# A graph layer on a sparse matrix: rows of A a unit ahead, list products before the addition, later stores, fewer open tiles, lists in pieces

## The chip, the cores and the metric

The kernel runs on one core of one Trainium2 chip. The metric is the device time of one launch in microseconds (us). The core has five engines with a queue of instructions each: PE (TensorE: matrix products and transposes), DVE (VectorE), ACT (ScalarE), POOL (GpSimd) and SP (SyncE, which only starts transfers and passes semaphores). Transfers between HBM and the on-chip memory run on 16 DMA engines; SP, ACT and POOL can ask for them. Products accumulate in eight PSUM banks of 128 x 512 fp32.

## The reference

With A the 4096 x 4096 input `adj`, x of shape 8 x 4096 x 256 and a 256 x 256 weight:

```python
HW = einsum('bnf,fo->bno', x, W)
A_norm = relu((A + A.T) * 0.5)
D = sum(A_norm, axis=1)
d = where(D > 0, D ** -0.5, 0)
L_norm = eye(N) - d[:, None] * A_norm * d[None, :]
out = relu(einsum('nm,bmo->bno', L_norm, HW))
return layernorm(x + out)          # over the last axis, eps 1e-5
```

A is sparse, and denser towards low node numbers: an entry (i, j) is kept with a chance that falls with both numbers. Where a block of A has no entry in a row, the product of that row can be left out.

## The kernel before

The nodes are cut into 32 blocks of 128 (NB). Every fp32 matmul stands in the trace as two records.

**The forming stage** runs over pairs (i, j) of 512 x 512 blocks, i from 0 to 7 and j from i to 7. For each pair two blocks of A are loaded on SP's queue (L455), transposed on PE (L465), added on DVE (`symmetrise`, L469), scaled and clipped on ACT (`keep`, L473) and written to `a_dram` on ACT's queue (L485). `keep` also sums each run of 32 columns on DVE (L476, `sums`); POOL marks which runs have an entry (`uses`, L477), and adds the runs in four halvings to one sum per row (L482 and L484, `part`), from which `degrees` makes the row factors. Between these, `form` multiplies x by W (L568, L579), scales it to g, writes it to `g_dram`, and `multiply` (L537) adds the dense first row block, `lead`. Nothing here is pinned to an order but by a few explicit dependencies: a planner orders each engine's instructions ahead of time. A list `due` holds work on lists, counted down once per pair (i, j) by `run_due`.

**Lists.** For every unit u, two row blocks 2u+1 and 2u+2 (the last has one), the kernel decides on the chip which nodes go where. `patterns` (L213) finds for every node which of the eight 32-column strips of the unit it touches; each pattern is a kind (KINDS). `count` and `count_rest` multiply these marks by triangular matrices on PE, `place` and `place_rest` turn the counts into slots on DVE (a scan, L205 to L210, then offers of overflow from one kind to another, L298 to L301, then the slot, L311 to L339), `spread` makes one-hot matrices, `collect` multiplies them, and `index` (L410 to L426) reads the resulting node numbers, `gi` and `ai`. CAPS gives how many half tiles of 64 nodes each kind has in each unit, FIRST at which half tile it begins. Both are constants; L186 and L187 write them to `limit` and `base` with one POOL memset for each unit and kind.

**The gathering stage** runs over units in the order SEQ. The first two or three node blocks (HUBS) are kept: their rows of g stay in `hubs`, and for each unit `load_hub_rows` loads their rows of A (`gh`, 128 x 256) on POOL's queue. All other nodes come in tiles of 128: `gather` (L904) asks for the tile's rows of A (`ga`, L910) and of g (`g`, L918) by indirect DMA into a ring of 11 slots, freed in order. `steps_of` lays out the products: a step is either one whole product (128 x 128, four matmuls over 2048 columns), or a round of up to eight products of 64 x 32, one per place of the array, taken from at most REACH open tiles. Two row blocks have four PSUM banks each, tag `b0` for the first and `b1` for the second. Within a round the two row halves of the array take turns at a bank; SP passes a tick from one quarter of the round to a later one (L1183), in SP's queue.

In this stage every engine keeps the order in which the code writes it (`queue`, `issue_after`). After each step `gather_ahead` refills free slots, and `run_later(2)` counts work that was put off down by two and runs what has come to two or less. When a row block is complete, `finish` has ACT evict it (L730), into one buffer `y`; `rest` then adds the residual and takes statistics on DVE (L740 to L768), `end` normalises (L773), and `store_late` stores on SP (L783). The residual lies in one of four buffers, which are loaded on ACT's queue (L724, `residuals`) and are free again when the store has landed. When the first row block of a unit is complete, `lists` runs the list products of later units on PE (two `b0` banks), and `read(False)` lets DVE read them (index, then both scans); `prepare` makes the one-hot matrices for the next.

Of the kernel before, what the change touches and what calls it, by code (L numbers as in the profile page):

```python
# [47 lines left out]
    [3, 6, 10, 13, 0, 22, 19, 24, 27, 16, 30, 50, 47, 44, 33],  # L48
    [9, 0, 6, 12, 3, 21, 27, 16, 24, 18, 42, 32, 40, 30, 34],
    [3, 8, 5, 11, 0, 25, 14, 20, 17, 23, 36, 38, 28, 30, 32],  # L50
    [3, 11, 8, 0, 6, 19, 24, 21, 14, 17, 26, 28, 35, 30, 32],
    [5, 7, 0, 9, 2, 12, 17, 20, 23, 15, 31, 26, 33, 30, 28],
    [12, 3, 6, 9, 0, 17, 14, 19, 24, 22, 28, 33, 32, 31, 29],
    [0, 2, 4, 7, 10, 14, 16, 19, 22, 25, 28, 29, 30, 31, 32],
    [9, 11, 6, 3, 0, 18, 23, 21, 14, 16, 26, 28, 30, 27, 29],
    [5, 3, 10, 7, 0, 21, 14, 18, 12, 16, 24, 26, 28, 27, 25],
    [3, 10, 8, 5, 0, 15, 17, 12, 19, 22, 24, 26, 27, 28, 25],
    [0, 4, 7, 9, 1, 18, 12, 14, 20, 17, 28, 24, 25, 26, 27],
    [3, 10, 4, 0, 7, 12, 19, 15, 22, 18, 26, 28, 27, 30, 29],
    [4, 6, 0, 2, 8, 17, 12, 10, 14, 19, 24, 20, 22, 23, 21],  # L60
    [8, 6, 4, 2, 0, 12, 16, 18, 10, 14, 20, 24, 22, 21, 23],
    [0, 2, 4, 6, 8, 10, 12, 14, 16, 18, 20, 20, 20, 21, 22],
    [0, 4, 8, 12, 16, 20, 20, 20, 20, 20, 20, 20, 20, 20, 20],
# [4 lines left out]
def kernel(  # L68
# [25 lines left out]
    nc = tc.nc  # L94
# [16 lines left out]
    REACH = 8  # L111
    LATE = 10
# [61 lines left out]
    carry = const.tile([P, NL, NB], F32, name="carry")  # L174
# [8 lines left out]
    for k in range(NL):  # L183
        nc.gpsimd.memset(kinds[:, k : k + 1], float(codes[k]))
        for u in range(NU):
            nc.gpsimd.memset(limit[:, u, k : k + 1], float(CAPS[u][k] * L))  # L186
            nc.gpsimd.memset(base[:, u, k : k + 1], float(FIRST[u][k] * L + 1))  # L187
# [78 lines left out]
    def place(u, tot, low):  # L266
# [36 lines left out]
        every = slice(None)  # L303
        for h in range(2):
            offer(0, (every, h), pairs)
# [3 lines left out]
        nc.vector.tensor_copy(upper[:, singles], upto[:, 2])  # L309
        fits = ipool.tile([P, NL, NB], F32, tag=f"incl{NL * NB}", name=f"fits_{u}", bufs=1)  # L310
# [129 lines left out]
    with (  # L440
# [10 lines left out]
        strips = holds.enter_context(tc.tile_pool(name="strips", bufs=8))  # L451
# [20 lines left out]
        def keep(i, j, sym, diag):  # L472
            nc.scalar.activation(sym, sym, AF.Relu, scale=0.5)  # L473
            rows = slice(i * A, (i + 1) * A)
            sums = stat1.tile([P, A, S // E], F32, tag="sums", name=f"sums_{i}_{j}", bufs=4)
# [4 lines left out]
            half = S // E // 2  # L480
            while half > 1:
                nc.gpsimd.tensor_add(sums[:, :, :half], sums[:, :, :half], sums[:, :, half : 2 * half])  # L482
                half //= 2
            nc.gpsimd.tensor_add(part[:, rows, j : j + 1], sums[:, :, :1], sums[:, :, 1:2])  # L484
# [144 lines left out]

        def count_place(u):  # L630
            tot = psum.tile([P, NL * NB], F32, tag="b0", name=f"tot_{u}")
            low = psum.tile([P, NL * NB], F32, tag="b0", name=f"low_{u}")
            count(u, tot, low)
            run(place(u, tot, low))
# [23 lines left out]
        for i in range(NS):  # L658
            diag = stat1.tile([P, A, P], F32, tag="diag", name=f"diag_{i}")
            for j in range(i, NS):  # L660
# [29 lines left out]
                run_due()  # L690
# [5 lines left out]
            if i == 1:  # L696
                for n, u in enumerate(SEQ[:2]):
                    patterns(u)
                    due += [[2 + n, count_place, (u,)], [4 + n, count_place_rest, (u,)]]
                due.sort(key=lambda d: d[0])  # L700
            elif i == 2:
                for n, u in enumerate(SEQ[2:4]):
                    patterns(u)
                    due.append([1 + n, count_place, (u,)])
                due.append([3, count_place_rest, (SEQ[2],)])
            elif i < 5 and i > 2:

                pieces = spread_early(SEQ[i - 3])
                for n in range(5):
                    due.append([1 + n // 2, next, (pieces, None)])  # L710
                due.append([4, collect_index, (SEQ[i - 3],)])
# [143 lines left out]
    with (  # L855
# [13 lines left out]
        hub_rows = [apool.tile([P, 2 * P], F32, tag=f"h{h}", name=f"gh{h}") for h in range(max(HUBS))]  # L869
# [22 lines left out]
        def load_hub_rows(units, h):  # L892

            u = next((v for v in units if HUBS[v] > h), None)
            if u is None:
                return
            with queue("pool"):
                nc.gpsimd.dma_start(
                    hub_rows[h], a_dram[h * P : (h + 1) * P, (2 * u + 1) * P : (2 * u + 3) * P]
                )  # L900
            got[u, -1 - h] = (hub_rows[h], hubs[h], P)
# [49 lines left out]
        for h in range(max(HUBS)):  # L951
            with queue("pool"):
                nc.gpsimd.dma_start(hubs[h], g_dram[h * P : (h + 1) * P, :])
            load_hub_rows(SEQ, h)
# [54 lines left out]
        def finish(i):  # L1009
# [24 lines left out]
            after(1, rest)  # L1034
# [24 lines left out]
        def lists(u):  # L1059
# [31 lines left out]
            after(1, read, False)  # L1091
# [18 lines left out]
        def product(u, op, c, ps, cols, start, stop):  # L1110

            t, _, b, _ = op
            at, gt, apart = got[u, t]
# [12 lines left out]
        for q, (u, step) in enumerate(steps):  # L1126
# [58 lines left out]
            for op in step:  # L1185
                t = op[0]
                uses_left[u, t] -= 1
                if t < 0 and not uses_left[u, t]:
                    load_hub_rows(SEQ[SEQ.index(u) + 1 :], -1 - t)
            gather_ahead()  # L1190
            run_later(2)
            for b in touched:
                if not any(left[b, e] for e in range(QU)):
                    finish(2 * u + 1 + b)
                    if b == 0:
                        after(2, lists, u)
        while later:
# [64 lines left out]
```

## Time and profile before

| what | us |
|---|---|
| median of 3 runs (lowest, highest) | 1694.35 (1692.22, 1695.94) |
| the profiled execution, its own time | 1692.59 |
| its span in the trace | 1690.8 |
| forming stage, up to the first product of L1116 | 616.6 |
| gathering stage, up to the end of PE's last product | 1050.6 |
| end (evictions, normalisation, last stores) | 23.6 |

| product group of L1116 | records | mean ns of one |
|---|---|---|
| 64 x 32 and whole, from the ring (`py<-g,ga`) | 7192 | 615 |
| whole, kept blocks (`py<-g_hub,gh`) | 592 | 643 |

The 7784 records of L1116 are the gathering stage. Their mean duration isn't the price of one, since up to eight run side by side; the price of a step is read from the timeline. In rows of the profile, the name before `<-` is what is written and the names behind it what is read; L-numbers are lines of the kernel printed above. A wait row names the engine and line that waited, what it waited for, the total in us, how often, and the longest. An engine's idle time matters only where the engine, or one that waits for it, sets the end.

### The profile page before, as it was taken

The numbers are of one execution on the slowest core, as the hardware profiler recorded it, in microseconds if no ns is written. First come the engines' busy times: TensorE is split into PE (matmuls) and PEld (weight loads), VectorE is DVE, ScalarE is ACT, GpSimd is POOL, SyncE is SP. The second block draws the span as 40 slices with busy tenths as digits, with TensorE's granted clock in tenths as the row PEclk, the third lists the DMA queues.
The fourth block names the chain that finished last, engine by engine and source line by source line (L and its number), as shares of the span: only waits on it lengthen the run. The fifth ranks groups of instructions, "written<-read, shape, count | busy, mean of one in ns | idle before, by whom it ended". The sixth has DMA issues, their size and how long they took to land.

```text
span 1690.8 us, 29762 instructions
## 1 busy us (share of the span) xinstructions
PE 1448.1 (86%) x11176; PEld 768.9 (45%) x11176; DVE 1022.9 (60%) x3071; ACT 367.2 (22%) x462; POOL 768.1 (45%) x1490
## 2 busy tenths in 40 slices
PE   5999989898889877989889789698999868879894
PEld 4788866676666632323223333243333323323331
DVE  4665689895464630092745938668047973975636
ACT  3555544444444510001010000100010010011002
POOL 5123121223233355656455375563546455647561
PEclk9999989999999988999999899898999979989997
DMA  8999999999888988889797788977859896999994
GB/s 309 373 368 399 386 342 339 353 319 362 299 301 320 367 319 311 342 308 367 280 357 285 276 307 300 368 278 290 331 209 384 287 359 223 333 341 357 353 385 146
DMA packets 217160, 546.74 MB, mean 323 GB/s; under 512 B 19035, under 2 KB 107403, under 8 KB 182955
## 3 DMA queue, kind: packets, MB, share of 16 engines
q0 software_dynamic: 54624, 286.49, 45.0%
q1 hardware_dynamic: 93472, 126.89, 21.9%
q10 hardware_dynamic: 68912, 131.37, 20.7%
q8 instruction: 91, 1.49, 0.3%
q14 instruction: 61, 0.50, 0.1%
HBM read 442.89 MB, written 136.34 MB: 343 GB/s over the span
## 4 chain that ended last, share of the span: by engine, by line
PE 46%; DVE 20%; DMA 17%; issue 8%; POOL 7%; ACT 2%; POOLq 0%; SPq 0%; ACTq 0%; DVEq 0%
PE py L1116 28%; PE pg L579 8%; DMA gh<-a_dram 5%; DMA g<-g_dram,gi 5%; PE lead L537 4%; DMA a_dram<-sym 4%; DVE sym L469 3%; DVE sums L476 2%; POOL g L918 2%; PE xtr L568 2%; PE tr L465 2%; POOL ga L910 2%; DMA ga<-a_dram,ai 2%; DVE stats L749 2%; DVE xr L773 1%
## 5 line engine op out<-in xcount | busy, mean ns | idle before, releaser
L1116 PE MATMUL py<-g,ga 64*32 64x512 f32 (+1 forms) x7192 | 603.7, 615 | 65.7 <-DMA g<-g_dram,gi 51.4
L1116 PEld LDWEIGHTS py<-g,ga 64*32 64x32 f32 (+1 forms) x7192 | 216.3, 113 | 440.0 <-issue 350.4
L910 POOL DMA_INDIRECT ga<-a_dram,ai x264 | 270.1, 1023 | 283.4 <-PE py L1116 218.1
L1116 PE MATMUL py<-g_hub,gh 128*128 128x512 f32 x592 | 293.1, 643 | 81.2 <-DMA gh<-a_dram 56.5
L918 POOL DMA_INDIRECT g<-g_dram,gi x264 | 292.6, 1108 | 103.6 <-issue 73.0
L740 DVE TENSOR_TENSOR xr<-xr,y 128x2048 f32<-128x2048 f32 x31 | 71.0, 2290 | 421.9 <-ACT y L730 421.9
L730 ACT ACTIVATE y<-py,minus_r 128x512 f32<-128x512 f32 x120 | 78.3, 687 | 958.3 <-PE py L1116 944.1
L579 PE MATMUL pg<-w_sb,xt 128*128 128x256 f32 x1024 | 232.7, 385 | 7.8 <-ACT xt L569 6.7
L1116 PEld LDWEIGHTS py<-g_hub,gh 128*128 128x128 f32 x592 | 115.8, 204 | 252.5 <-issue 148.6
L469 DVE TENSOR_TENSOR sym<-tr,adj 128x512 f32<-128x512 f32 x256 | 162.6, 682 | 93.7 <-PE tr L465 73.7
L579 PEld LDWEIGHTS pg<-w_sb,xt 128*128 128x128 f32 x1024 | 195.9, 194 | 36.4 <-ACT xt L569 7.1
L476 DVE TENSOR_REDUCE sums<-sym 128x64 f32<-128x2048 f32 x64 | 145.4, 2279 | 66.5 <-ACT sym L473 66.5
L465 PE MATMUL tr<-ident,adj 128*128 128x128 f32 x1024 | 140.2, 286 | 40.6 <-DVE sym L469 26.6
L473 ACT ACTIVATE sym<-sym 128x2048 f32<-128x2048 f32 x64 | 122.5, 1915 | 147.4 <-DVE sym L469 132.7
L477 POOL TENSOR_SCALAR uses<-sums 128x64 uint8<-128x64 f32 x64 | 28.1, 439 | 273.4 <-DVE sums L476 228.7
L465 PEld LDWEIGHTS tr<-ident,adj 128*128 128x128 f32 x1024 | 119.1, 146 | 72.3 <-DVE sym L469 41.7
L568 PE MATMUL xtr<-ident,xin 128*128 128x128 f32 x512 | 72.7, 286 | 20.5 <-DVE sym L469 19.3
L749 DVE BATCH_NORM_STATS2 stats<-xr 128x6 f32<-128x256 f32 x256 | 87.0, 412 | 1.1
L773 DVE TENSOR_SCALAR xr<-xr,mv,root 128x256 f32<-128x256 f32 x248 | 85.1, 415 | 0.1
L537 PE MATMUL lead<-gt,strip 128*128 128x512 f32 x176 | 83.0, 598 | 0.0
L569 ACT COPY xt<-xtr 128x512 f32<-128x512 f32 x128 | 68.0, 590 | 46.5 <-PE xtr L568 45.6
L589 ACT ACTIVATE gt<-pg,r 128x512 f32<-128x512 f32 x88 | 60.6, 688 | 75.0 <-PE pg L579 72.8
(153 smaller groups left out, 997.4 us busy)
## 6 DMA issues: line engine op xcount, KB each, us to landing
adj<-in_adj_dram SPq DMA_DIRECT2D x64, 1024.0 KB, 11.0
a_dram<-sym ACTq DMA_DIRECT2D x64, 1024.0 KB, 9.5
out_dram<-xr SPq DMA_DIRECT2D x31, 1024.0 KB, 5.6
xr<-in_x_dram ACTq DMA_DIRECT2D x29, 1024.0 KB, 18.1
xin<-in_x_dram SPq DMA_DIRECT2D x44, 512.0 KB, 12.6
g_dram<-gt ACTq DMA_DIRECT2D x22, 1024.0 KB, 7.2
xin<-in_x_dram POOLq DMA_DIRECT2D x20, 512.0 KB
g_dram<-held ACTq DMA_DIRECT2D x10, 1024.0 KB, 10.5
```

The costliest lines, as they stand in the source:

```text
L465: ins = nc.tensor.transpose(pt[:, c * P : (c + 1) * P], tji[:, c, a * P : (a + 1) * P], ident)
L469: nc.vector.tensor_add(sym[:, a, :], pt, tij[:, a, :])
L473: nc.scalar.activation(sym, sym, AF.Relu, scale=0.5)
L476: nc.vector.tensor_reduce(sums, sym.rearrange("p a (c q) -> p a c q", q=E), AX.X, ALU.add)
L537: nc.tensor.matmul(lead[c], lhsT=strip, rhs=g[:, c * S : (c + 1) * S], start=not done, stop=len(done) == NB - 1, skip_group_check=True,)
L568: nc.tensor.transpose(pt[:, k, c, :], xin[b // H][:, b % H + k, c * P : (c + 1) * P], ident)
L579: ins = nc.tensor.matmul(pg[:, k * FO : (k + 1) * FO], lhsT=xt[:, b + k, c, :], rhs=w_sb[:, c, :], start=(c == 0), stop=(c == FC - 1),)
L749: nc.vector.bn_stats(stats[:, b, :], z[:, b, :])
L773: nc.vector.tensor_scalar(z[:, b, :], z[:, b, :], mv[:, b, 0:1], rstd[:, b : b + 1], ALU.subtract, ALU.mult,)
L910: nc.gpsimd.indirect_dma_start(out=at if both else at[:, :P], out_offset=None, in_=a_pairs if both else a_rows, in_offset=bass.IndirectOff ...
L918: nc.gpsimd.indirect_dma_start(out=gt, out_offset=None, in_=g_dram, in_offset=bass.IndirectOffsetOnAxis(ap=gi[:, t : t + 1], axis=0), boun ...
L1116: return nc.tensor.matmul(py[2 * u + 1 + b][c][cols, :], lhsT=at[ps, off + cols.start : off + cols.stop], rhs=gt[ps, c * S : (c + 1) * S], ...
```

## The change

It does the following, and nothing else:

- Each kept block's rows of A are two tiles of 128 x 128, one for each row block of a unit. `load_hub_rows` is called after every last use of such a half, for the next unit that keeps this block.
- `lists` is put off before `finish`, `rest` is put off by two instead of one (both come after the next step, the lists now first), and `read(False)` runs at once instead of a step later.
- LATE is 18 instead of 10. REACH is 5 instead of 8. FIRST is another order of the kinds within the tiles; CAPS stays. The number of gathered tiles stays at 264.
- In the forming stage `run_due` runs after each block instead of each pair of blocks, `place` yields at two more points, and `patterns`, `place` and `place_rest` of the first four units are due one after the other; `spread` and `collect_index` have new due times.
- The row sums of `sums` are one DVE reduction instead of four POOL additions. `strips` has 10 buffers instead of 8, `sums` 3 instead of 4, `carry` is BF16. `limit` and `base` are written unit by unit in the order SEQ.

```diff
-    REACH = 8
-    LATE = 10
+    REACH = 5
+    LATE = 18
...
-    carry = const.tile([P, NL, NB], F32, name="carry")
+    carry = const.tile([P, NL, NB], BF16, name="carry")
...
-        for u in range(NU):
+    for u in SEQ:
+        for k in range(NL):
             nc.gpsimd.memset(limit[:, u, k : k + 1], float(CAPS[u][k] * L))
             nc.gpsimd.memset(base[:, u, k : k + 1], float(FIRST[u][k] * L + 1))
...
         every = slice(None)
+        yield
         for h in range(2):
             offer(0, (every, h), pairs)
...
         nc.vector.tensor_copy(upper[:, singles], upto[:, 2])
+        yield
...
-        strips = holds.enter_context(tc.tile_pool(name="strips", bufs=8))
+        strips = holds.enter_context(tc.tile_pool(name="strips", bufs=10))
...
-            half = S // E // 2
-            while half > 1:
-                nc.gpsimd.tensor_add(sums[:, :, :half], sums[:, :, :half], sums[:, :, half : 2 * half])
-                half //= 2
-            nc.gpsimd.tensor_add(part[:, rows, j : j + 1], sums[:, :, :1], sums[:, :, 1:2])
+            nc.vector.tensor_reduce(part[:, rows, j], sums, AX.X, ALU.add)
...
+        begun_lists = {}
+
+        def more(u):
+            next(begun_lists[u], None)
+
         def count_place(u):
...
-            run(place(u, tot, low))
+            begun_lists[u] = place(u, tot, low)
+            more(u)
...
                     keep(rows, cols, sym, diag)
-                run_due()
+                    run_due()
...
-            if i == 1:
-                for n, u in enumerate(SEQ[:2]):
-                    patterns(u)
-                    due += [[2 + n, count_place, (u,)], [4 + n, count_place_rest, (u,)]]
-                due.sort(key=lambda d: d[0])
-            elif i == 2:
...
+            if i in (1, 2):
+                for n, u in enumerate(SEQ[2 * i - 2 : 2 * i]):
+                    at = 1 + 5 * n
+                    due += [[at, patterns, (u,)], [at + 1, count_place, (u,)]]
+                    due += [[at + 2 + k, more, (u,)] for k in range(3)]
+                    if (i, n) != (2, 1):
+                        due.append([at + 5, count_place_rest, (u,)])
+            elif i in (3, 4):
                 pieces = spread_early(SEQ[i - 3])
-                for n in range(5):
-                    due.append([1 + n // 2, next, (pieces, None)])
-                due.append([4, collect_index, (SEQ[i - 3],)])
+                due += [[at, next, (pieces, None)] for at in (1, 2, 3, 3, 4)]
+                due.append([5, collect_index, (SEQ[i - 3],)])
+            due.sort(key=lambda d: d[0])
...
-        hub_rows = [apool.tile([P, 2 * P], F32, tag=f"h{h}", name=f"gh{h}") for h in range(max(HUBS))]
+        hub_rows = [
+            [apool.tile([P, P], F32, tag=f"h{h}{b}", name=f"gh{h}_{b}") for b in range(2)] for h in range(max(HUBS))
+        ]
...
-        def load_hub_rows(units, h):
+        def load_hub_rows(units, h, b):
...
+            i = 2 * u + 1 + b
             with queue("pool"):
                 nc.gpsimd.dma_start(
-                    hub_rows[h], a_dram[h * P : (h + 1) * P, (2 * u + 1) * P : (2 * u + 3) * P]
+                    hub_rows[h][b], a_dram[h * P : (h + 1) * P, i * P : (i + 1) * P]
                 )
...
-            after(1, rest)
+            after(2, rest)
...
-            after(1, read, False)
+            read(False)
             after(6, read, True)
...
-                if t < 0 and not uses_left[u, t]:
-                    load_hub_rows(SEQ[SEQ.index(u) + 1 :], -1 - t)
+                if t < 0:
+                    load_hub_rows(SEQ[SEQ.index(u) + 1 :], -1 - t, op[2])
             gather_ahead()
             run_later(2)
             for b in touched:
                 if not any(left[b, e] for e in range(QU)):
-                    finish(2 * u + 1 + b)
                     if b == 0:
                         after(2, lists, u)
+                    finish(2 * u + 1 + b)
```

FIRST before and after, for the first unit of SEQ (u = 1) as an example; all others but that of u = 14 change likewise:

```diff
-    [9, 0, 6, 12, 3, 21, 27, 16, 24, 18, 42, 32, 40, 30, 34],
+    [9, 0, 3, 6, 12, 18, 21, 16, 27, 24, 32, 30, 40, 42, 34],
```

## What I expected of it, before seeing the result

> **What bounds the kernel now.** I read the page first (engine totals, slices, costliest groups), then the waits, then windows and the timeline where the waits fall.
>
> ```profile
> PE 1448.1 (86%) x11176; PEld 768.9 (45%) x11176; DVE 1022.9 (60%) x3071; ACT 367.2 (22%) x462; POOL 768.1 (45%) x1490
> ...
> 10.00:18.00 8.00, 1.27 (x6) 0.87 (x5) 0.00 (x0) 0.00 (x0) 7.21 (x217) 0.83 0.96 335
> 18.00:26.00 8.00, 6.06 (x40) 5.79 (x40) 7.98 (x15) 4.66 (x4) 1.99 (x32) 0.74 0.48 145
> 120.00:200.00 80.00, 78.97 (x453) 64.62 (x452) 48.04 (x56) 42.43 (x53) 22.63 (x70) 1.00 1.05 397
> 616.00:1667.00 1051.00, 904.11 (x8284) 347.66 (x8282) 621.06 (x2300) 81.57 (x125) 583.24 (x563) 0.93 0.86 315
> ```
>
> The window rows give PE, PEld, DVE, ACT and POOL busy, the granted clock, the DMA share and GB/s. PE is the longest engine. The forming stage (to 616 us) runs PE and DMA together near their limits at 120 to 200. The gathering stage, 1051 us, has PE busy 904 us and DMA at 0.86: neither is full.
>
> ```profile
> 728.02 3.66 PE L1116 MATMUL py<-g,ga 64*32 64x512 f32 x64
> 1133.78 0.35 PE L263 MATMUL lists<-kind,ones 128*128 128x448 bf16 x1
> 1135.02 3.68 PE L1116 MATMUL py<-g,ga 128*128 128x512 f32 x8
> 1138.54 7.03 PE L1116 MATMUL py<-g_hub,gh 128*128 128x512 f32 x16
> ```
>
> These give the price of a step. A whole product (8 records) and a round of eight small ones (64 records) take the same, 1138.54 - 1135.02 = 3.52 us from start to start; the list products take 1135.02 - 1133.78 = 1.24 us. CAPS and FIRST, put through steps_of, give 118 whole products and 115 rounds with 855 small products: 8 x (118 + 855) = 7784 records, as many as L1116 has in the table above. So PE needs 233 x 3.52 + 15 x 1.24 = 839 us, and about 210 of the 1051 us are waits and slow steps.
>
> ```profile
> PE py L1116 <- DMA gh<-a_dram: 56.5, 9, 11.9
> PE py L1116 <- DMA g<-g_dram,gi: 51.4, 17, 6.6
> ...
> PE py L1116 <- DVE pos_k L209: 24.0, 7, 6.6
> ...
> PE py L1116 <- SPq L1183: 11.9, 3, 7.3
> ```
>
> Four waits (us, times, longest) make 143.8 of it. The rest is slow steps after a wait:
>
> ```profile
> 953.28 5.71 PE L1116 MATMUL py<-g_hub,gh 128*128 128x512 f32 x8 [7.50 <-DMA gh<-a_dram]
> ...
> 1156.77 6.36 PE L1116 MATMUL py<-g_hub,gh 128*128 128x512 f32 x8 [7.61 <-DMA gh<-a_dram]
> 1162.96 3.60 PE L1116 MATMUL py<-g,ga 128*128 128x512 f32 x8
> ...
> 1571.21 5.65 PE L1116 MATMUL py<-g_hub,gh 128*128 128x512 f32 x8 [5.03 <-DMA gh<-a_dram]
> ...
> 1157.00:1163.00 6.00, 6.00 (x9) 2.42 (x10) 5.90 (x18) 0.00 (x0) 0.00 (x0) 0.57 1.02 390
> 1163.00:1170.00 7.00, 7.00 (x25) 2.89 (x31) 6.56 (x21) 0.00 (x0) 0.00 (x0) 1.00 0.43 154
> ```
>
> After 7.61 us idle the granted clock is 0.57, and the next step takes 6.36 us instead of 3.60. The first and the last of the seven gh waits over 5 us stand around it.
>
> **The change, part by part.** All against the profiled execution: 1690.8 us of span and 1.8 outside it, 1692.6, which is 1.8 below the median of 1694.35.
>
> *Rows of A for the kept tiles.* Today one tile holds both halves, so the next unit's rows are asked for only after the second half's last product, near the unit's end, and then stand behind gathers:
>
> ```profile
> 1147.09 0.60 POOL L898 DMA_DIRECT2D gh<-a_dram x1
> 1147.99 1.02 POOL L910 DMA_INDIRECT ga<-a_dram,ai x1 [0.30 <-issue]
> 1149.31 1.00 POOL L918 DMA_INDIRECT g<-g_dram,gi x1 [0.31 <-DMA g<-g_dram,gi]
> ```
>
> The request at 1147.09 landed at 1156.77, 9.7 us. After the change the first half is asked for after its own last use, in the first steps of a unit, and used a unit later, as the second half is: by the step lists eight steps (28 us) or more for both. That exceeds 9.7 us by far: **-56.5**. The seven long waits of the nine carry a slow step, 2.1 to 2.8 us too long in the three rows, 2.4 taken for each: **-17**. Added: 37 more requests of 0.60 + 0.30 us on POOL, 33 us over the stage beside 583 us busy in 1051. Most fall in a unit's first steps, where POOL waits for ring slots: nothing; uncovered, up to +33. The Trainium skill ("DMA: Bandwidth & Descriptors", section on the anatomy of one DMA, SWDGE path) gives each such DMA a fixed cost of about 2.0 us; were that serial, 37 x 2.0 = 74 us would come back. The trace does not agree: POOL's gathers (264 of ga in the row below and as many of g) would need 1056 us of fixed costs alone, more than the whole stage, so they overlap.
>
> ```profile
> L910 POOL DMA_INDIRECT ga<-a_dram,ai x264 | 270.1, 1023 | 283.4 <-PE py L1116 218.1
> ```
>
> *List products ahead of the addition.* Now the list reads stand behind a finished block's addition and statistics on DVE, and the two banks that they hold are wanted by the next unit's first product:
>
> ```profile
> 1131.04 2.29 DVE L740 TENSOR_TENSOR xr<-xr,y 128x2048 f32<-128x2048 f32 x1 [12.43 <-ACT y L730]
> ...
> 1139.17 0.16 DVE L410 COPY low<-lists 128x15 f32<-128x15 f32 x1
> ...
> 1142.54 0.62 DVE L210 TENSOR_TENSOR pos_k<-pos_k,lists 128x448 f32<-128x448 f32 x1
> ```
>
> DVE waits with the reads until the products are done (1135), reads for 1143.16 - 1139.17 = 4 us, and is through at about 1139 instead of 1143.16, before the next unit in all units but one, where a single step lies between. **-21** of 24.0. Behind the waiting read on DVE stand the addition and statistics, some 8 us later than now; behind them ACT's eviction of the unit's other block (one y buffer), which nobody needs until step 4 of the next unit, 14 us. Nothing; uncovered, 3 us a unit, +45.
>
> *Later stores.*
>
> ```profile
> SPq L783 <- DVE xr L773: 54.6, 6, 15.0
> ```
>
> SP waits up to 15 us with a store for the normalisation, and the ticks of L1183 that PE's rounds wait for stand behind it. 18 instead of 10, counted down by two a step, is four steps later, 14 us: **-12** (11.9). Cover gone: 0. The price is residual buffers held longer, a rival below.
>
> *Fewer tiles open, new FIRST.*
>
> ```profile
> 630.21 1.88 PE L1116 MATMUL py<-g,ga 64*32 64x512 f32 x2 [6.27 <-DMA g<-g_dram,gi]
> ...
> 639.33 5.64 PE L1116 MATMUL py<-g,ga 64*32 64x512 f32 x58 [4.55 <-DMA g<-g_dram,gi]
> ...
> 678.67 34.55 PE L1116 MATMUL py<-g,ga 64*32 64x512 f32 x330 [3.71 <-DMA g<-g_dram,gi]
> ...
> 1472.05 15.77 PE L1116 MATMUL py<-g,ga 64*32 64x512 f32 x234 [5.35 <-DMA g<-g_dram,gi]
> ```
>
> Counted again: 121 whole products, 116 rounds: 4 more steps, **+14** (4 x 3.52). For each tile I counted the steps between the release of its ring slot and its first use. Of those after the first unit's opening, 19 had three steps or fewer before, 9 do after. The gather waits without the opening's three (11.6 us) are 39.8; the seven over 2.5 us, from the third row to the last, bring slow steps of some 2 us like those above, 14. Scaled by 9/19, 54 becomes 25: **-29**. The opening needs five tiles instead of six, one gather of 1.13 MB at the 397 GB/s above: **-3**.
>
> ```profile
> 996.00:1016.00 20.00, 20.00 (x196) 7.95 (x181) 10.55 (x41) 2.42 (x4) 14.64 (x15) 1.00 1.03 411
> 1216.00:1236.00 20.00, 20.00 (x229) 7.44 (x214) 0.00 (x0) 0.00 (x0) 5.51 (x6) 1.00 0.41 147
> ...
> POOL ga L910 <- PE py L1116: 218.1, 75, 17.1
> ```
>
> Some of that is given back. DMA swings between 411 and 147 GB/s because POOL waits 218 us for ring slots. Units 9 to 11 load 46 tiles of about 1.13 MB, and 13.7 MB of residuals, stores and kept rows: 65.6 MB, 162 us at 405 GB/s, against 37 steps and three lists, 134 us. The ring's eleven tiles (31 us at most) cover about half of the 28: **+13**.
>
> *Start and forming stage.*
>
> ```profile
> 18.02 0.17 DVE L279 TENSOR_TENSOR ends<-base,limit 128x14 f32<-128x14 f32 x1 [15.48 <-POOL base L187]
> ...
> 19.07 5.17 PE L465 MATMUL tr<-ident,adj 128*128 128x128 f32 x32 [7.80 <-DVE sym L469]
> ...
> L482 POOL TENSOR_TENSOR sums<-sums 128x32 f32<-128x32 f32 (+2 forms) x192 | 47.5, 247 | 15.0
> ...
> L496 DVE TENSOR_REDUCE deg<-part 128x4 f32<-128x32 f32 x8 | 1.5, 184 | 9.1 <-POOL part L484 9.1
> ```
>
> DVE stands until 18.02 for the last memset of the first unit's row. With units outermost it is written after 14 + 28 of 462 memsets, so PE's 7.80 us wait goes; DMA was busy till 18 and half idle after (0.48 of 8 us), so between 4 and 8: **-6**. POOL loses L482's 47.5 us of adds and their last stage, off the path; DVE gains 64 reduces, twice L496's elements, 0.2 us each, 13 us; L496's 9.1 us wait goes. List work in pieces over twice as many turns should take some of the PE waits on DVE between 200 and 530 away; two more strip buffers help at the end. Together between +12 (reduces uncovered) and -30; near the small end, as PE and DMA are both close to full: **-8**. The BF16 carry and three sums buffers: nothing, at most 1 us either way.
>
> **Sum:** -56.5 - 17 - 21 - 12 + 14 - 29 - 3 + 13 - 6 - 8 = -125.5, so 1692.6 - 125.5 = **1567 us**.
>
> **Rivals.**
>
> *Transfers become the limit.* The stage's DMA work is 0.86 x 1051 = 904 us of full share; the forecast leaves about 1051 - 111 = 940 us, a share of 0.96. For it: bursts at 1.03 beside PE waits for g. Against: 80 us at 1.05 with PE 99% busy. If only 0.92 can be held, the stage takes 983 us: 1610.
>
> *Gather waits go too*: with slots freed evenly the 25 + 13 us left vanish, and the forming stage gives 20 rather than 8: 1517.
>
> *The halves come no earlier*: POOL takes its queue in order, and if the new requests end up behind full-ring waits (218.1 us), 56.5 + 17 stay: 1641. By the Trainium skill's fixed cost, 74 us serial, the time would be the same 1641; the two share a chance.
>
> *Residual loads hit the later stores (slower).* ACT issues the load of a block, waits for its buffer, and the evictions stand behind it, and PE behind those. Now a store comes with the eighth step of the following unit, after the change with the twelfth; the load reusing its buffer comes with the fifth step of the unit after. By the count four steps (14 us) remain in the shortest case, where one landing takes 5.6 us:
>
> ```profile
> out_dram<-xr SPq DMA_DIRECT2D x31, 1024.0 KB, 5.6
> ```
>
> It decides once DVE is four steps late with normalisations. ACT would then hold PE some 10 us in 14 units for good: 140 + 8 lost against the gain: about 1715.
>
> *Nothing that can be measured*: every wait removed reappears as a gather wait: 1693.
>
> **How the numbers follow.** Forecast 0.54; transfers the limit 0.22; gather waits go 0.12; halves no earlier, or their cost serial, 0.06; residuals 0.03; nothing 0.03. The range goes from the third case to just past the second, with the stage 10 us worse: 1517 to 1620. The bounds of the parts (+33, +45, +12) lie inside it one at a time. This kernel's times differ by about 0.2%, which a measurement cannot tell from no change. Faster 0.94, same 0.03, slower 0.03.
>
> **What would show each step.** The wait for gh gone, and gh issues spread in two per kept tile; the wait for pos_k under 5 us, with low and incl_k ahead of xr on DVE; no wait of PE for SPq over 1 us; PE waits for g at 20 to 45 us, the largest in units 9 to 11 and where a round comes two steps after its slot; the first sym addition near 9 us; the gathering stage 930 to 950 us with a DMA share of 0.95. I am wrong if the g wait grows past 90 us, if ACT shows waits before y for an out_dram landing, or if the stage below 616 us moves by more than 30.

## The result and the profile after

| | before | after |
|---|---|---|
| median of 4 runs (lowest, highest), us | 1693.28 (1690.54, 1695.94) | 1553.44 (1552.23, 1554.03) |
| span of the profiled execution, us | 1690.8 | 1552.2 |
| forming stage | 616.6 | 594.2 |
| gathering stage | 1050.6 | 931.3 |
| end, after PE's last product | 23.6 | 26.7 |

The ratio is 0.9173, with a 95% interval of 0.9156 to 0.919: 140 us saved where the sum of the forecast was 125.5. The stages differ by -22.4, -119.3 and +3.1 us. First the page of the changed kernel: the engine totals.

```profile
span 1552.2 us, 29354 instructions
PE 1428.7 (92%) x11008; PEld 766.6 (49%) x11008; DVE 1040.1 (67%) x3135; ACT 364.0 (23%) x462; POOL 744.4 (48%) x1271
```

PE did nearly the same work (1428.7 us busy, 1448.1 before) in a shorter span. The window of the gathering stage of the changed kernel (busy us of PE, PEld, DVE, ACT, POOL, then granted clock, DMA share, GB/s):

```profile
594.00:1525.00 931.00, 887.41 (x8115) 344.05 (x8113) 620.40 (x2287) 78.15 (x125) 620.43 (x596) 0.97 0.95 356
```

The DMA share rose from 0.86 to 0.95, GB/s from 315 to 356, and the granted clock from 0.93 to 0.97: PE stands less often, and there are fewer slow steps after a wait (a record of the kept blocks' products took 643 ns in the mean and now 599). The page's groups of products and of the gathers on POOL in the changed kernel:

```profile
L1121 PE MATMUL py<-g,ga 64*32 64x512 f32 (+1 forms) x7024 | 614.6, 608 | 40.9 <-DMA g<-g_dram,gi 37.8
L914 POOL DMA_INDIRECT ga<-a_dram,ai x264 | 284.7, 1079 | 160.4 <-PE py L1121 86.2
L1121 PE MATMUL py<-g_hub,gh 128*128 128x512 f32 x592 | 267.4, 599 | 1.7 <-DVE pos_k L210 1.7
```

```profile
PE py L1121 <- SPq L1188: 0.2, 1, 0.2
```

The idle time ahead of the kept tiles' products was 81.2 us before and is 1.7. The wait for gh (56.5) isn't there at all, the one for pos_k fell from 24.0 to 1.7, the one for SP's ticks from 11.9 to 0.2, the one for gathers from 51.4 to 37.8. POOL's wait for free ring slots fell from 218.1 to 86.2. 7024 + 592 = 7616 = 8 x (121 + 831) records, as counted ahead: 121 whole products and 116 rounds.

The start of the changed kernel in the timeline (start, duration, then engine and instruction), to be held against the three rows of the prediction's part on the start:

```profile
3.43 0.17 DVE L280 TENSOR_TENSOR ends<-base,limit 128x14 f32<-128x14 f32 x1 [0.86 <-POOL base L188]
8.78 0.69 DVE L472 TENSOR_TENSOR sym<-tr,adj 128x512 f32<-128x512 f32 x1 [0.85 <-PE tr L468]
...
13.43 3.87 PE L468 MATMUL tr<-ident,adj 128*128 128x128 f32 x32 [2.13 <-DMA adj<-in_adj_dram]
```

DVE no longer waits for a memset until 18.02; the first addition is at 8.78, and PE waits 2.13 us for a load where it waited 7.80 for DVE.

### The profile page after: what moved, and what is told of

It reads as the page before. It is cut to its first block, busy times and chain, and to the rows that moved or that the text cites. A ratio compares the mean times of both kernels' runs of the same rounds, so it can differ in the third digit from the quotient of the medians.

```text
span 1552.2 us, 29354 instructions
## 1 busy us (share of the span) xinstructions
PE 1428.7 (92%) x11008; PEld 766.6 (49%) x11008; DVE 1040.1 (67%) x3135; ACT 364.0 (23%) x462; POOL 744.4 (48%) x1271
## 3 DMA queue, kind: packets, MB, share of 16 engines
q10 hardware_dynamic: 68912, 131.37, 22.4%
## 4 chain that ended last, share of the span: by engine, by line
PE 61%; DMA 16%; DVE 13%; issue 5%; POOL 3%; ACT 1%; SPq 0%; ACTq 0%; POOLq 0%; DVEq 0%
PE py L1121 40%; PE pg L578 9%; DMA g<-g_dram,gi 5%; PE lead L536 5%; DVE sym L472 4%; DMA out_dram<-xr 3%; PE xtr L567 3%; PE tr L468 3%; DMA xin<-in_x_dram 3%; DVE sums L479 3%; DMA a_dram<-sym 2%; POOL ga L914 1%; DMA ga<-a_dram,ai 1%; DMA xr<-in_x_dram 1%; ACT sym L476 1%
## 5 line engine op out<-in xcount | busy, mean ns | idle before, releaser
L1121 PE MATMUL py<-g,ga 64*32 64x512 f32 (+1 forms) x7024 | 614.6, 608 | 40.9 <-DMA g<-g_dram,gi 37.8
L1121 PEld LDWEIGHTS py<-g,ga 64*32 64x32 f32 (+1 forms) x7024 | 219.6, 112 | 420.7 <-issue 331.4
L914 POOL DMA_INDIRECT ga<-a_dram,ai x264 | 284.7, 1079 | 160.4 <-PE py L1121 86.2
L922 POOL DMA_INDIRECT g<-g_dram,gi x264 | 296.6, 1123 | 105.7 <-issue 64.0
L731 ACT ACTIVATE y<-py,minus_r 128x512 f32<-128x512 f32 x120 | 75.6, 687 | 836.1 <-PE py L1121 694.0
L1121 PE MATMUL py<-g_hub,gh 128*128 128x512 f32 x592 | 267.4, 599 | 1.7 <-DVE pos_k L210 1.7
L1121 PEld LDWEIGHTS py<-g_hub,gh 128*128 128x128 f32 x592 | 109.3, 190 | 154.8 <-issue 146.1
L479 DVE TENSOR_REDUCE sums<-sym 128x64 f32<-128x2048 f32 x64 | 145.4, 2278 | 54.4 <-ACT sym L476 54.4
L567 PE MATMUL xtr<-ident,xin 128*128 128x128 f32 x512 | 73.4, 294 | 14.5 <-DVE sym L472 12.8
## 6 DMA issues: line engine op xcount, KB each, us to landing
out_dram<-xr SPq DMA_DIRECT2D x31, 1024.0 KB, 22.9
xr<-in_x_dram ACTq DMA_DIRECT2D x29, 1024.0 KB, 16.2
g_dram<-held ACTq DMA_DIRECT2D x10, 1024.0 KB, 11.9
```

The source lines that it names most:

```text
L479: nc.vector.tensor_reduce(sums, sym.rearrange("p a (c q) -> p a c q", q=E), AX.X, ALU.add)
L567: nc.tensor.transpose(pt[:, k, c, :], xin[b // H][:, b % H + k, c * P : (c + 1) * P], ident)
L914: nc.gpsimd.indirect_dma_start(out=at if both else at[:, :P], out_offset=None, in_=a_pairs if both else a_rows, in_offset=bass.IndirectOff ...
L922: nc.gpsimd.indirect_dma_start(out=gt, out_offset=None, in_=g_dram, in_offset=bass.IndirectOffsetOnAxis(ap=gi[:, t : t + 1], axis=0), boun ...
L1121: return nc.tensor.matmul(py[2 * u + 1 + b][c][cols, :], lhsT=at[ps, off + cols.start : off + cols.stop], rhs=gt[ps, c * S : (c + 1) * S], ...
```

## The experiments

**Theory:** each part of the change takes out the wait named for it, so each is worth about its own term (halves of A -73.5, lists -21, later stores -12, tiles and FIRST -5, start and forming stage -14), and the terms add up. **Rival:** the parts lean on each other. A wait of PE that goes is paid back by another one through an engine that both share, so that a part alone gains less than its term, or loses, and two together more.

Each experiment undoes one part of the changed kernel, or puts one part on the kernel before. Ratios are against the kernel before on the same chip. The base time to compare with is the changed kernel run once more:

**The changed kernel again (ctl).** No edit.

> The changed kernel itself, as a measure for the runs beside it. If this chip behaves as in the first comparison: 1553, ratio 0.917. If the ticks from SP are as slow here as in the four runs before (PE waited 182 to 202 us for them, in every version): near 1800, ratio 0.955 to 0.965, and parts can only be told apart by their waits.

1552.85 us against 1696.97, ratio 0.9156 (0.9115 to 0.9196).

**Halves alone, on the kernel before (o_hub).**

```diff
-        hub_rows = [apool.tile([P, 2 * P], F32, tag=f"h{h}", name=f"gh{h}") for h in range(max(HUBS))]
+        hub_rows = [
+            [apool.tile([P, P], F32, tag=f"h{h}{b}", name=f"gh{h}_{b}") for b in range(2)] for h in range(max(HUBS))
+        ]
...
-                if t < 0 and not uses_left[u, t]:
-                    load_hub_rows(SEQ[SEQ.index(u) + 1 :], -1 - t)
+                if t < 0:
+                    load_hub_rows(SEQ[SEQ.index(u) + 1 :], -1 - t, op[2])
```

> The kernel before, with only the rows of A of the kept blocks in two halves. Theory (waits add up): the gh wait of 56.5 and the slow steps of 17 go, nothing else moves: 1693 - 73 = 1620, ratio 0.957. Rival 1 (PE then waits for g or for the list reads where it waited for gh): the gh wait is 0 but the g or pos_k wait grows by 30 or more, about 1655. Rival 2 (each of the 37 more requests costs a serial 2 us): 1693.

1653.21 us, ratio 0.9737 (0.9699 to 0.9774): -43.8 us, not -73.5. The waits of PE in it (total, times, longest):

```profile
PE py L1120 <- DMA g<-g_dram,gi: 60.4, 19, 8.7
...
PE py L1120 <- DVE pos_k L209: 24.0, 7, 6.3
PE py L1120 <- SPq L1187: 23.6, 7, 6.0
```

The wait for gh is gone, all 56.5 us of it. But the wait for SP's ticks doubled, 11.9 to 23.6, and that for gathers went from 51.4 to 60.4: 20.7 us came back in other places. In the profiled executions the four named waits fell by 35.8 us together and the gathering stage by 39.6 (1050.6 to 1011.0), so by this estimate only some 4 of the 17 us put on slow steps were saved. What SP itself waits for says why the ticks are late:

```profile
SPq L783 <- DVE xr L773: 73.6, 8, 14.1
```

PE reaches the next unit's rounds sooner; SP still stands with a store, waiting for DVE's normalisation (54.6 us before, 73.6 now), and the ticks are behind that store in its queue.

**Halves and lists, on the kernel before (o_hublists).** The edit above, and:

```diff
-            after(1, rest)
+            after(2, rest)
...
-            after(1, read, False)
+            read(False)
...
-                    finish(2 * u + 1 + b)
                     if b == 0:
                         after(2, lists, u)
+                    finish(2 * u + 1 + b)
```

> The kernel before with the rows of A in two halves and with the list products and reads ahead of the addition; stores, FIRST and the forming stage as before. The halves alone gave 1653 (ratio 0.974). Theory: the pos_k wait of 24 falls under 3, 1653 - 21 = 1632, ratio 0.962. Rival (the normalisations come later, SP stands longer behind the stores, and PE's wait for ticks, 23.6 with the halves alone, takes the gain): 1645 to 1655.

1689.39 us, ratio 0.9962 (0.9942 to 0.9981). Against halves alone (on another chip, so by the ratios) it is 0.0225 higher, 38 us: the list edit alone, meant to save 21, **costs** 38. Its waits of PE:

```profile
PE py L1120 <- SPq L1187: 95.8, 12, 15.0
...
PE py L1120 <- DVE pos_k L209: 3.0, 2, 1.5
```

and those of SP:

```profile
SPq L783 <- DVE xr L773: 149.7, 14, 21.4
```

pos_k fell from 24.0 to 3.0, as the edit is meant to do. But now the waits of SP for the normalisation come 14 times instead of 8, for 149.7 us, and PE waits 95.8 us for ticks. That is the rival named ahead of the run, but far larger than the 1645 to 1655 us that it was given.

**The changed kernel with early stores (u_late2).**

```diff
-    LATE = 18
+    LATE = 10
```

> The changed kernel with LATE 10, on a chip where its ticks are fast. Theory of the prediction: PE's wait for SP's ticks comes back with 12 us, 1565. Rival 1 (units are shorter and normalisations later now, so that far more stores are awaited): 25 to 45 us in the SPq waits, 1580 to 1600. Rival 2 (the tail gains back what the ticks lose): 1553.

1661.6 us, ratio 0.9787 (0.9769 to 0.9805): 104 to 109 us worse than the changed kernel (by the ratios of the two runs of it, and by medians). That is far beyond the 25 to 45 us of the rival as well. With all the rest in place, one constant, to which the prediction gave 12 us, is worth this much. The waits of PE, and of SP:

```profile
PE py L1121 <- SPq L1188: 133.6, 12, 14.0
...
PE py L1121 <- DMA g<-g_dram,gi: 15.3, 7, 6.5
```

```profile
SPq L784 <- DVE xr L774: 181.6, 14, 21.8
```

One such wait can be followed through the timeline of this kernel:

```profile
915.25 0.18 DVE L413 COPY low<-lists 128x17 f32<-128x17 f32 x1 [25.88 <-PE lists L401]
...
919.04 2.28 DVE L741 TENSOR_TENSOR xr<-xr,y 128x2048 f32<-128x2048 f32 x1
...
930.01 2.28 DVE L741 TENSOR_TENSOR xr<-xr,y 128x2048 f32<-128x2048 f32 x1
...
950.12 4.63 DVE L380 TENSOR_TENSOR hot<-iota_q,at 128x1024 bf16<-128x1024 f32 x4
...
959.53 2.67 DVE L774 TENSOR_SCALAR xr<-xr,mv,root 128x256 f32<-128x256 f32 x8
```

```profile
936.65 25.95 SPq L784 DMA_DIRECT2D out_dram<-xr  x2
```

```profile
948.16 1.94 PE L1121 MATMUL py<-g,ga 64*32 64x512 f32 x28 [0.27 <-DMA g<-g_dram,gi]
962.71 3.67 PE L1121 MATMUL py<-g,ga 64*32 64x512 f32 x32 [12.61 <-SPq L1188]
```

Read it from the top. DVE stands 25.88 us with the list read, until PE's list products are there. Behind that read come, in the order of the code, one block's addition (919.04), its statistics and normalisation, the other block's addition (930.01), then list work up to 959.53 (the scans, the one-hot matrices of L380), and only then the second normalisation, which ends at 962.20. SP's two stores of L784 stand in the second row: the first leaves at 936.65, the second is through at 962.60. PE has stopped at 950.10 in the middle of a round whose tick is behind that store, and goes on at 962.71. No product waits for this normalisation, and yet it holds PE for 12.61 us through a queue that only passes ticks. Four steps more of LATE put the store behind those ticks.

**Two steps later instead of four (late14).** The stores of the two blocks before the final one are early as well, to see whether the end gets shorter:

```diff
-    LATE = 18
+    LATE = 14
...
-                    after(LATE, store_late)
+                    after({NB - 3: 6, NB - 2: 4}.get(i, LATE), store_late)
```

> The changed kernel with LATE 14, and the last two blocks before the final one stored three and two steps after their normalisation instead of after the final block's stores. Theory: residual loads, which stand 18 to 21 us on ACT's queue for a buffer in the last units of the changed kernel, come 7 us sooner, the last addition does not wait, and the end from PE's last product, 26.7 us, falls by 6 to 9; ticks stay clean: about 1545. Rival 1 (14 is too early for the ticks): SPq waits of 5 us or more, 1553 to 1560. Rival 2 (the end is set by the final block's own chain): within 2 us of 1553.

1583.86 us, ratio 0.9336 (0.9321 to 0.9352): 28 to 31 us worse. The sign of rival 1 came, at four times its price or more.

```profile
PE py L1121 <- SPq L1188: 38.0, 7, 7.1
...
PE py L1121 <- DMA g<-g_dram,gi: 28.6, 15, 6.2
```

The three values of LATE (the middle one with the two early stores) stand in a row: 10, 14, 18 give waits of SP for the normalisation of 181.6, 54.4 and 7.8 us, waits of PE for ticks of 133.6, 38.0 and 0.2, and times of 1662, 1584 and 1553 us. Meanwhile the wait of PE for gathers goes the other way, 15.3, 28.6, 37.8: transfers catch up while PE stands for something else. The end after PE's last product was 21.7 us here, 26.7 and 26.0 in the two runs of the changed kernel. Early stores of the last blocks with LATE left at 18 were not tried, so whether those 5 us can be had without the 28 stays open.

**FIRST and REACH alone, on the kernel before (o_first).**

```diff
-    REACH = 8
+    REACH = 5
```

and FIRST as after.

> The kernel before, with only the new FIRST and REACH 5. Theory: waits for g and their slow steps fall by 29, the opening by 3, four more steps cost 14: 1693 - 18 = 1675. Rival 1 (the waits at the units' start had hidden the gathers, so nothing falls): only the 14 of the steps, 1707. Rival 2 (the open tiles were what held the ring): the g wait falls below 20, about 1650.

1680.82 us, ratio 0.989 (0.9836 to 0.9944): -16 us by the medians, from -28 to -9 by the interval of the ratio.

```profile
PE py L1116 <- DMA g<-g_dram,gi: 28.6, 10, 6.2
PE py L1116 <- SPq L1183: 27.9, 7, 7.4
```

The wait for gathers fell from 51.4 to 28.6, the one for ticks rose from 11.9 to 27.9: here too a wait for ticks takes part of the gain.

**FIRST and REACH undone in the changed kernel (u_first2).** The same edit the other way round.

> The changed kernel with the old FIRST and REACH 8, on a chip where its ticks are fast. Theory: as on the kernel before, where they gave 16, 1569. Rival 1 (with PE faster the ring is under more strain, open tiles cost more): 25 to 40 us, the g wait of 40 at 65 or more, about 1585. Rival 2 (transfers set the pace whatever is open): within 5 us.

1573.53 us, ratio 0.9271 (0.9241 to 0.93): 17 to 21 us worse. PE's wait for gathers is 64.0 us in 25 times (37.8 in 18 with the new FIRST); there is none for ticks in the list of its waits.

**The forming stage as before, in the changed kernel (u_form).** The list work in its old pieces and order, POOL's additions, eight strips, four sums, memsets in the old order; the carry stays BF16. The core of it:

```diff
-    for u in SEQ:
-        for k in range(NL):
+        for u in range(NU):
...
-            nc.vector.tensor_reduce(part[:, rows, j], sums, AX.X, ALU.add)
+            half = S // E // 2
+            while half > 1:
+                nc.gpsimd.tensor_add(sums[:, :, :half], sums[:, :, :half], sums[:, :, half : 2 * half])
+                half //= 2
+            nc.gpsimd.tensor_add(part[:, rows, j : j + 1], sums[:, :, :1], sums[:, :, 1:2])
...
-                    run_due()
+                run_due()
```

> The changed kernel with the forming stage as before: memsets in the old order, POOL additions, list work once per pair in the old pieces, 8 strip and 4 sums buffers (carry stays BF16). Theory: the 22 us that the forming stage lost come back in that stage alone, 1575. Rival (the stage is bound by transfers anyway, and the start alone counts): 6 to 10 us, 1562.

1576.36 us, ratio 0.9288 (0.9254 to 0.9321), 23.5 us worse than the changed kernel beside it. In the profiled executions (1581.1 us, and 1552.78 for the changed kernel) the first product of the gathering stage starts at 622.98 and at 593.05. This execution of u_form is the slowest of its four by more than 4 us, but its 28.3 us over the other all lie in this stage (29.9). Its waits of PE for DVE's addition of the transposes:

```profile
PE tr L467 <- DVE sym L471: 27.5, 18, 8.0
...
PE xtr L570 <- DVE sym L471: 17.4, 13, 4.5
```

In the changed kernel beside it:

```profile
PE tr L468 <- DVE sym L472: 17.1, 17, 4.0
...
PE xtr L567 <- DVE sym L472: 12.4, 9, 2.7
```

15.4 us of the difference are in these two rows (27.5 - 17.1 and 17.4 - 12.4). The longest single wait of them, 8.0 us, is that of the start, behind the memsets; only the other 7.4 can come from list work in small pieces, which would hold DVE's additions for shorter stretches. Which of the forming stage's edits brought how much was not separated by a run.

**Four runs that could not tell the parts apart.** The first four experiments ran on a chip on which the kernel before takes 1884.87 us (1869.55 to 1891.54), and their times are compared with that alone. Each undoes one part of the changed kernel: the halves in one tile (u_hub), the old list order (u_lists), LATE = 10 (u_late), the old FIRST with REACH = 8 (u_first); the edits are those above, the other way round.

> The changed kernel, but each kept block's rows of A are again one tile for both halves, asked for after the last use of both. Theory (waits add up): the wait for gh and its slow steps come back, 56.5 + 17 us on 1553, about 1627. Rival (while PE stands for gh, the ring fills, so that PE then waits less for g): the gh wait comes back but the g wait of 37.8 falls by some 20 to 30 us, about 1600. If the time stays under 1570, the halves were not what counted.

> The changed kernel, but with the list products and their reads in the old order: finish ahead of lists, rest one step later, first reads a step after the products. Theory: PE waits again for pos_k at the units' first step, 24 us as before, about 1575. Rival 1 (units are shorter now, so DVE is later against PE): 35 to 45 us, about 1595. Rival 2 (without the gh wait the reads come in time): no more than 5 us.

> The changed kernel with LATE 10 instead of 18. Theory: SP stands behind stores again, PE's wait for SPq returns with about 12 us, 1565. Rival 1 (the normalisation now comes later, behind the list reads, so stores wait longer): 20 to 40 us, about 1580. Rival 2 (it mattered only beside the old order of FIRST): under 4 us.

> The changed kernel with the old FIRST and REACH 8. Theory: 4 steps fewer (-14), the waits for g with their slow steps back (+29), the opening (+3): about 1571. Rival (the transfers set these waits, not the open tiles): the 4 steps fewer show, 1540 to 1553.

| | us | ratio (95%) | PE waits for SP's ticks, us (times) |
|---|---|---|---|
| u_hub | 1816.39 | 0.9639 (0.9579, 0.9699) | 193.8 (71) |
| u_lists | 1826.2 | 0.9679 (0.9618, 0.974) | 181.6 (65) |
| u_late | 1830.54 | 0.9717 (0.9658, 0.9776) | 202.4 (75) |
| u_first | 1820.43 | 0.9644 (0.9578, 0.9709) | 182.2 (79) |

The expectations in us were missed throughout, and the four intervals overlap. A wait for ticks in 65 to 79 pieces lies over all of them; on the other chips no version has it more than 12 times. Only signs that don't depend on the total can be read. With the old list order PE again waits for pos_k, as the theory said; with LATE = 10 SP again waits for the normalisation, 105.8 us in 11 times, which no list of the other three has. But with the halves in one tile the wait for gh comes back with 8.1 us in three times, not with 56.5: what the halves are worth inside the changed kernel stays open.

```profile
PE py L1121 <- SPq L1188: 181.6, 65, 10.5
...
PE py L1121 <- DVE pos_k L210: 25.9, 8, 5.6
```

What the wait consists of is told in the last section. LATE and FIRST were therefore run again on another chip (u_late2, u_first2).

**The parts together:**

| part | the prediction's terms | measured | in which surroundings |
|---|---|---|---|
| halves | -73.5 | -43.8 | alone, on the kernel before |
| list products ahead | -21 | +38 | on halves, with LATE 10 |
| later stores | -12 | -104 to -109 | with all the rest |
| tiles, FIRST, REACH | -5 (+14 - 29 - 3 + 13) | -16; -17 to -21 | alone; with all the rest |
| start and forming stage | -14 | -23.5 | with all the rest |

The rival holds: the terms don't add up one by one. By the difference to the whole (1552.85 - 1696.97 = -144.1, less 43.8, 16.2 and 23.5) lists and later stores are worth some -60 together, where one of them alone costs 38 us. This -60 is what is left over, not a run of its own, and it mixes surroundings; later stores on the kernel before, without the rest, were not tried. No version that was run beats the changed kernel.

## Why the prediction was right, and where it was not

The time, 1553, is 14 us below the forecast of 1567 and inside its range.

**Rows of A.** The mechanism held. The wait for gh is gone, at once and by itself (o_hub). The term was mis-sized: -56.5 - 17 is what the waits and slow steps cost in the trace of before, not what their removal gives, and 20.7 us came back as waits for ticks and gathers, and most of the 17 us for slow steps was not saved. The serial price for the 37 added requests isn't there. POOL issues all of them in the changed kernel at the same price as before:

```profile
L902 POOL DMA_DIRECT2D gh<-a_dram x74 | 43.1, 585 | 31.3 <-PE py L1121 20.0 <-DMA ga<-a_dram,ai 5.3 <-DVE half L767 2.9
```

o_hub has those requests too and gained 43.8 us. The fixed cost of about 2.0 us for one DMA ("DMA: Bandwidth & Descriptors" of the Trainium skill, section on the anatomy of one DMA) would by an estimate, one after the other, need 2.0 x (264 + 264 + 74) = 1204 us. The stage took 931 us, so on POOL's queue these costs overlap here.

**List products ahead.** pos_k fell to 1.7, under the 5 us forecast. The step that failed is "Behind the waiting read on DVE stand the addition and statistics, some 8 us later than now; behind them ACT's eviction of the unit's other block ... Nothing". It followed the queue to ACT and stopped there. The normalisation is also behind the read, SP's store waits for it, and the ticks for PE stand behind the store: 38 us with LATE at 10. The later addition in the changed kernel, in the timeline:

```profile
1044.20 0.15 DVE L413 COPY low<-lists 128x15 f32<-128x15 f32 x1
...
1048.10 2.28 DVE L741 TENSOR_TENSOR xr<-xr,y 128x2048 f32<-128x2048 f32 x1
...
1056.42 2.67 DVE L774 TENSOR_SCALAR xr<-xr,mv,root 128x256 f32<-128x256 f32 x8
```

The list read comes first, then the addition, then the normalisation. The waits of other engines that this order makes are long and cost nothing:

```profile
DVE low L413 <- PE lists L401: 247.4, 13, 70.3
ACT y L731 <- DVE xr L741: 142.0, 15, 11.0
```

So the "uncovered, +45" on ACT did not come true.

**Later stores.** "-12 (11.9). Cover gone: 0" is the largest error. The direction was right, and SP's wait is all but gone in the changed kernel:

```profile
SPq L784 <- DVE xr L774: 7.8, 4, 4.3
```

But 11.9 us was the wait in a kernel in which seven units waited 5 to 12 us for gh, and whose normalisations came earlier. As those went and the list reads moved ahead of the normalisation, the same stores cost PE more and more: 23.6 us with the halves alone (o_hub), 95.8 with the lists too (o_hublists), 133.6 with all but the later stores (u_late2). That the total came out near is in part luck, because errors are opposite: the halves gave 30 us less by themselves, while lists -21 and stores -12 were to give -33 and gave about -60 together, and the last two terms gave some 20 more.

**Tiles and FIRST.** The four more steps are there (7616 records), and the wait for gathers is 37.8 us, which the prediction put at 20 to 45. The first, the longest and the last of the 18, in the timeline of the changed kernel:

```profile
606.99 1.88 PE L1121 MATMUL py<-g,ga 64*32 64x512 f32 x2 [5.50 <-DMA g<-g_dram,gi]
...
979.83 12.29 PE L1121 MATMUL py<-g,ga 64*32 64x512 f32 x130 [6.47 <-DMA g<-g_dram,gi]
...
1513.83 11.67 PE L1121 MATMUL py<-g,ga 64*32 64x512 f32 x108 [1.42 <-DMA g<-g_dram,gi]
```

The opening's three waits came to 8.9 us (5.50 the first) instead of 11.6 (6.27 the first), so its -3 held. The longest, 6.47, is in unit 6, not in units 9 to 11, where the prediction expected it because of their many transfers; those have eight, of 0.34 to 3.43, 12.8 us together. The net of -5 was too small by 11 to 16 us; whether the -29 or the +13 was off, the runs don't say.

**Start and forming stage.** The first addition came at 8.78 us, as said (near 9). The stage lost 22.4 us instead of 14, and u_form gives 23.5: the term was mis-sized by 8 us or more. By stretches with the same PE records (1064, then 1273 or 1274, then 561) the two profiled executions say where: to 208.0 us before and 204.0 after, 4 us for the start where 6 were forecast; then 272.0 against 258.0 us, 14 in the stretch in which DVE does the list work (from 225.72 and 223.63 us); then 136.6 against 132.2. So the part after the start gave some 18 instead of 8, within its own bounds of +12 and -30. In the middle stretch the DMA share went from 0.91 to 0.96: it was less full than "PE and DMA are both close to full" had it.

**Transfers as the limit.** The share reached 0.95, as the forecast needed, and did not stop at 0.92; the stage took 931 us (930 to 950 were forecast).

**Residual loads.** This rival decided nothing, but its margin was overrated: "one landing takes 5.6 us" became

```profile
out_dram<-xr SPq DMA_DIRECT2D x31, 1024.0 KB, 22.9
```

and ACT's issue of two residuals stands some 20 us, to the very moment of the next eviction:

```profile
1475.94 20.78 ACTq L725 DMA_DIRECT2D xr<-in_x_dram  x2
1496.83 2.42 ACT L731 ACTIVATE y<-py,minus_r 128x512 f32<-128x512 f32 x4 [32.84 <-PE py L1121]
```

1475.94 + 20.78 = 1496.72. The prediction named as a sign against it "ACT shows waits before y for an out_dram landing". In this execution the profile puts that idle time down to PE; in the other profiled execution of the same kernel the same place, with the same 20 us of issue, is put down to the landing, in the list of its waits:

```profile
ACT y L731 <- DMA out_dram<-xr: 63.8, 2, 32.3
```

So the sign came, without the loss: in the lists of PE's waits there is one for an eviction of L731, 1.1 us in the one execution and 0.2 in the other, before a list product. DVE does wait for residuals, 23.6 us in three times, all in the last units. Here are the last of these and DVE's last addition of that kind:

```profile
1501.88 2.29 DVE L741 TENSOR_TENSOR xr<-xr,y 128x2048 f32<-128x2048 f32 x1 [10.50 <-DMA xr<-in_x_dram]
...
1519.42 2.29 DVE L741 TENSOR_TENSOR xr<-xr,y 128x2048 f32<-128x2048 f32 x1 [6.31 <-issue]
```

DVE stands 6.31 us before its last addition, and the profile names nothing that it waits for ("issue"). The block's eviction was done at 1506.69 (1504.27 + 2.42), so the residual, asked for by 1496.72, is the likely reason. The end after PE's last product, which the prediction left as it was, is 3.1 us longer. That the one causes the other is likely by the order of the rows, but no run took it apart.

## What to carry to other kernels

Follow a delayed instruction through every queue until nobody waits any more, queues that only pass semaphores included: here DVE's normalisation held a store on SP, and the store held ticks that PE's next round needed. The wait that a trace shows is the price at the present timing, not the worth of its removal: 11.9 us became 133.6 once PE no longer stood for other reasons and the normalisation came later, so price parts that share a queue together. When a part of a change makes things worse alone (+38 us here), run it with the part that may cover it before dropping it.

## What the hardware showed that was not expected

A store's landing got slower as the transfers got fuller. The same 1 MB stores of `out_dram` took a median of 5.6 us from issue to landing at a DMA share of 0.86 in the gathering stage (kernel before), 11.2 at 0.89 (o_hub), 21.1 at 0.92 (late14) and 22.9 at 0.95 (changed kernel). The share alone doesn't set it: three runs at 0.87 had 5.2 (o_first), 6.9 (u_late2) and 12.5 us (o_hublists), and what else does stays open.

On one chip the ticks came late. With the old list order there, the timeline has

```profile
1433.65 2.34 PE L1121 MATMUL py<-g,ga 64*32 64x512 f32 x16 [1.93 <-SPq L1188]
...
1443.00 1.96 PE L1121 MATMUL py<-g,ga 64*32 64x512 f32 x16 [7.01 <-SPq L1188]
```

and, for those 7 us, in the window:

```profile
1436.00:1443.00 7.00, 0.00 (x0) 0.00 (x0) 0.00 (x0) 0.00 (x0) 5.48 (x6) 0.50 1.01 392
```

PE, DVE and ACT do nothing from 1435.99 to 1443, no store stands in SP's way, and every product before the wait had ended by 1435.99. SP's own list puts 66 of its waits down to no engine of the trace ("remote"):

```profile
SPq L1188 <- remote: 316.3, 66, 14.6
```

Why a tick takes 7 us there stays open; the trace doesn't show it. On the other chips the kernel before takes 1693 to 1697 us, and there is no such row.
